# A graph layer's gathers and single rows: 128 rows in every second gather, and single rows loaded in three parts instead of two

## The chip, the cores and the metric

One core of a Trainium2 chip runs the program. The metric is the device time of one execution in microseconds. Four executions of the kernel before took 15,992.88 to 15,995.08 us, median 15,993.74 us. A further execution was taken by the profiler; the trace and the page come from it.

## What is computed

A graph of 50,000 nodes with 128 features and 1,650,000 edges, sorted by target node. Each edge carries its source's row, multiplied by one of two weight matrices, to its target; the sums go through relu, the input is added, and each row is normalized.

```python
Xs = X[src]
m_data = Xs @ W_data.T + b_data
m_ctrl = Xs @ W_control.T + b_control
msg = jnp.where((edge_types == 0)[:, None], m_data, m_ctrl)
agg = jax.ops.segment_sum(msg, dst, num_segments=X.shape[0])
out = jax.nn.relu(agg + (X @ W_self.T + b_self))
x = _layernorm(x + out, axis=-1)
```

Every node also has one edge to itself (a self-loop) among the 1,650,000.

## The kernel before, in words

The kernel sums source rows first and multiplies by the weights afterwards. The edges are cut into blocks of 3234 in their sorted order, so 511 blocks (`NBLK`): 510 full ones and a rest of 7 gathers. A block is two steps (`Q`) of 1617 edges, and a step's edges come to the core in three ways:

- **Gathers.** Twelve (`R`) indirect DMAs on GpSimd's queue (`gathers`, L467, issued at L473) fetch 126 rows each (`SIZES`, L45) into a tile `y`. Six gathers share one slot of ten (`SLOTS`) and form a pass (`PASS`); four passes make a block. TensorE multiplies each gathered set with a one-hot matrix of targets and types (`products`, L484, matmul L492) into `acc`.
- **Fillers.** A self-loop needs no gather, since the node's own row is in the core anyhow. So its place in the gather lists is given to another edge's source: `fill` (L306) puts `F` = 41 edges per step in the places of 41 self-loops among the gathered ones. VectorE does it five blocks ahead (`RAHEAD`), in operations over 26 × 41 = 1066 elements (L316 to L335). Fewer self-loops than F in any step would send the program through a second, general path as well (L568, L936).
- **Single rows.** `S` = 64 edges per step come as 64 ordinary DMAs of 512 bytes. SP's queue issues the first 32 of a step and ScalarE's the other 32 (`TURN`, L423), two blocks ahead (`AHEAD`). `single_rows` (L435) loads 32 row offsets from the SBUF tile `at_x` into registers in one instruction (L442, `TENSOR_LOAD`), then issues 32 DMAs from these registers (L447: a `MOVE` and the DMA for each). VectorE writes the offsets, in bytes, in `offsets` (L433), at the end of the block before. Before the step's last matmul TensorE waits for all of the block's rows (`rows_fetched`, L452) and adds them with one matmul (L498).

`manual_schedule` means that every engine runs its instructions in the order in which the program writes them. The loop at L607 writes, for block b: on SP the load of a later block's own rows (`window`, L403); then, spread over the four passes q = 0 to 3, at q = 0 the weights of block b − 1 (`layer`, TensorE), its mean and variance (`moments`, VectorE), the one-hot matrix of block b + 2 (L409) and single rows of block b + 2, step 0; at q = 1 the square root of block b − 1 on ScalarE (`root`, L547) and the counts (L417); at q = 2 `store` of block b − 1 (VectorE's reciprocal L553 and normalization L555, which need the square root, then the store by SP, L556), the fillers of block b + 5, and single rows of block b + 2, step 1; at q = 3 the offsets of block b + 3. So ScalarE's queue holds, block after block: load, 32 rows, square root, load, 32 rows. SP's holds: own rows, load, 32 rows, store, load, 32 rows.

One more place loads several values into registers: `window` (L397) loads the first nodes of five blocks into SP's registers, in every fifth block; the last time one value is left.

```python
_, regs = nc.values_load_multi_w_load_instructions(
    base_i[0:1, b:b + n], engines=[SP], min_val=0, max_val=N - B,
```

Of the kernel before, what the change touches and what calls it, by code (L numbers as in the profile page):

```python
# [2 lines left out]

# [10 lines left out]
U8 = mybir.dt.uint8  # L14
# [10 lines left out]
ROW = 4 * D  # L25
E = 1650000
P = 128
# [6 lines left out]
R = 12  # L34
W = 60
Q = 2
PASS = 6
B = 112
C = R * Q
F = 41  # L40
S = 64
X = Q * S
R1 = R + 1
C1 = Q * R1
SIZES = [126] * R  # L45
SIZE = sum(SIZES)
CE = Q * SIZE
BE = CE + Q * F + X
NBLK = 2 + (E - CE) // BE
REST = E - CE - (NBLK - 2) * BE  # L50
REST_ROWS = [min(n, max(0, REST - q * SIZE - sum(SIZES[:r]))) for q in range(Q) for r, n in enumerate(SIZES)]
RCH = sum(n > 0 for n in REST_ROWS)
assert len(SIZES) == R and sum(REST_ROWS) == REST
GB = 10
GROUPS = -(-NBLK // GB)
GC = GB * C1
AHEAD = 2
# [17 lines left out]
TBL = GROUPS * GB  # L75
# [3 lines left out]
def plain(b):  # L79

    return b == 0 or b >= NBLK - 1
# [6 lines left out]
def straight(ctx, tc, c, x, x_t, src_t, dst_t, etype_t, src_f, dst_f, etype_f, src_x, dst_first, first_p, out):  # L88
# [13 lines left out]
    nc = tc.nc  # L102
# [21 lines left out]
                   allow_small_or_imprecise_dtypes=True)  # L124
    FILL = Q * F + C1
    small = keep_ps.tile([P, 2 * W + F + 2 * FILL + 2], F32, name="small")
    num_ps, rank_no_ps = small[:, :2 * W], small[:, 2 * W:2 * W + F]
    lists = [small[:, 2 * W + F + i * FILL:][:, :FILL] for i in range(2)]
    sums_at = [small[:Q * F, 2 * W + F + 2 * FILL + i:][:, :1] for i in range(2)]

# [80 lines left out]
    def clear_sums():  # L211
        for t in sums:
            nc.vector.memset(t, 0.0)
            nc.vector.memset(t[0:3, 2, :], 1.0)
            nc.vector.memset(t[0:2, 2, :], 0.0)
# [80 lines left out]
    def spread_out(g):  # L296
        vd_g[g] = dram.tile([GS * F], F32, name="vd")
        nc.sync.dma_start(vd_g[g].rearrange("(s f) -> s f", f=F), vp_g.pop(g))
# [39 lines left out]
    def left_out_columns(b):  # L338

        if not plain(b):  # L340
            pc = sums_at[b % 2]
            nc.tensor.matmul(pc, bys.pop(b).rearrange("p q f -> p (q f)"), ones_b[:, 0:1], start=True, stop=True)  # L342
            pcs[b] = pc

    def left_out_matrix(b):
        if not plain(b):
            z = fil.tile([Q * F, 2, P], BF16, name="z", bufs=RAHEAD + 1)
            at = fil.tile([Q * F, 1], F32, name="at")
            nc.vector.tensor_copy(at, pcs.pop(b))
            nc.vector.tensor_scalar(z.rearrange("p t n -> p (t n)"), node_no, at, None, op0=ALU.is_equal)  # L350
            zs[b] = z
# [22 lines left out]
    def column(k):  # L374
        return k // R * R1 + k % R

    def steps_of(b):
        return [q for q in range(Q) if len(chunks_of(b, q))]
# [8 lines left out]

    idxs = {0: idx0}
    bys, pcs, zs, pls, bases, ats, ys = {}, {}, {}, {}, {}, {}, {}
    ohs, cnts, accs, xTs, pos, hs, mvs, sds = {}, {}, {}, {}, {}, {}, {}, {}  # L390

    BASES = 5

# [12 lines left out]
    def onehot(b):  # L406
        g, i = divmod(b, GB)
        oh = ohp.tile([P, C1, 2 * W], F32, name="oh")
        nc.vector.tensor_tensor(oh, col_g[g][:, i, :, None].to_broadcast([P, C1, 2 * W]),  # L409
                                num_ps[:, None, :].to_broadcast([P, C1, 2 * W]), op=ALU.is_equal)  # L410
        ohs[b] = oh

    def counts(b):

        cnt = ohp.tile([P, Q, 2 * W], BF16, name="cnt")
        with nc.allow_low_precision(reason="whole numbers up to R1"):
            nc.vector.tensor_reduce(cnt, ohs[b].rearrange("p (q r) w -> p q w r", r=R1), AX.X, ALU.add)  # L417
        cnts[b] = cnt
# [1 line left out]


    ROW_SLOTS = AHEAD + 2
    TURN = S // 2  # L423
    RANGE = dict(min_val=0, max_val=(N - 1) * ROW, skip_runtime_bounds_check_because="where a node's row is")
    x_bytes = x.rearrange("n d -> (n d)").bitcast(U8)[None, :]
    fetched = [[tc.alloc_semaphore(f"fetched{j}_{i}") for i in range(ROW_SLOTS)] for j in range(2)]
# [5 lines left out]
            ats[b] = stp.tile([1, X], I32, name="at_x", bufs=AHEAD + 2)  # L432
            nc.vector.tensor_scalar(ats[b], one_g[g][:, i * X:(i + 1) * X], float(ROW), None, op0=ALU.mult)  # L433

    def single_rows(b, q):  # L435

        if q == 0:
            ys[b] = stp.tile([S, Q, D], F32, name="yx", bufs=ROW_SLOTS)
        both = []
        for j, (eng, dma) in enumerate(((SP, nc.sync), (ACT, nc.scalar))):  # L440
            at = j * TURN
            _, rows = nc.values_load_multi_w_load_instructions(  # L442
                ats[b][0:1, q * S + at:q * S + at + TURN], engines=[eng], **RANGE)
            both.append([(dma, fetched[j][b % ROW_SLOTS], at + k, row) for k, row in enumerate(rows)])
        for pair in zip(*both):
            for dma, sem, k, row in pair:
                copy = dma.dma_start(ys[b][k:k + 1, q, :].bitcast(U8), x_bytes[:, bass.ds(row, ROW)])  # L447
                copy.then_inc(sem, 16)
                tc.no_tile_sem_insts.add(copy.ins.name)
                tc.add_to_no_dep_group(f"single{b}", copy.ins)  # L450

    def rows_fetched(b):  # L452

        times = len(range(b % ROW_SLOTS or ROW_SLOTS, b + 1, ROW_SLOTS))
        for j in range(2):
            wait = nc.tensor.wait_ge(fetched[j][b % ROW_SLOTS], 16 * Q * TURN * times)
        tc.declare_fence(wait.ins, group=f"single{b}")


# [7 lines left out]
    def gathers(b, ks):  # L467
# [3 lines left out]
        for k in ks:  # L471
            r = REST_ROWS[k] if b == NBLK - 1 else SIZES[k % R]
            copy = nc.gpsimd.indirect_dma_start(  # L473
# [10 lines left out]
    def products(b, q, ks):  # L484
# [5 lines left out]
        for k in ks:  # L490
            r = REST_ROWS[k] if b == NBLK - 1 else SIZES[k % R]
            nc.tensor.matmul(acc[:, :2, :].rearrange("p t w -> p (t w)"), y[:r, k % PASS, :], ohs[b][:r, column(k), :],  # L492
                             start=k == of_step[0], stop=plain(b) and k == of_step[-1])
        if ks[-1] == of_step[-1]:
            if not plain(b):
                if q == 0:
                    rows_fetched(b)
                nc.tensor.matmul(acc[:, :2, :].rearrange("p t w -> p (t w)"), ys[b][:, q, :],  # L498
                                 ohs[b][:S, q * R1 + R, :], start=False, stop=True)
            for t in range(2):  # L500
# [49 lines left out]
    def store(b):  # L550
        mv = mvs.pop(b)
        rstd = stp.tile([B, 1], F32, name="rstd")
        nc.vector.reciprocal(rstd, sds.pop(b))  # L553
        o = stp.tile([B, D], F32, name="o")
        nc.vector.tensor_scalar(o, hs.pop(b), mv[:, 0:1], rstd, op0=ALU.subtract, op1=ALU.mult)  # L555
        nc.sync.dma_start(out[bass.ds(bases.pop(b), B), :], o)  # L556

    def find_bad():

# [36 lines left out]
    for b in range(1, RAHEAD):  # L596
        fill(b)
        left_out_columns(b)
        left_out_matrix(b)
        if b < AHEAD:  # L600
            onehot(b)
            counts(b)
            for q in range(Q):
                single_rows(b, q)
        if b == 1:
            clear_sums()
    for b in range(NBLK + 1):  # L607
        if b == NBLK - 1:
            find_bad()
        if b + 3 < NBLK:  # L610
            window(b + 3)
        g, i = divmod(b, GB)
        if i == 0 and g + 1 < GROUPS:
            load_edges(g + 1)
        if i == 3 and g + 1 < GROUPS:
            spread_out(g + 1)
        if i == 4 and g + 1 < GROUPS:
            spread_in(g + 1)
        if b > 0:
            add(b - 1, steps_of(b - 1)[-1])  # L620
        if b < NBLK:
            begin_sums(b)
        last = steps_of(b)[-1:]
        for q, (step, ks) in enumerate(passes_of(b)):
            if ks:
                products(b, step, ks)
            if q == 0 and b > 0:
                layer(b - 1)
            if q == 1:
                left_out_numbers(b + 1)  # L630
            if q == 3:
                left_out_columns(b + RAHEAD)
            if ks and step not in last and ks[-1] == chunks_of(b, step)[-1]:
                add(b, step)
            if q == 0 and b > 0:
                moments(b - 1)
            if q == 0 and b + AHEAD < NBLK:
                onehot(b + AHEAD)
            if q == 1 and b > 0:
                root(b - 1)  # L640
            if q == 2 and b > 0:
                store(b - 1)
            if q == 1 and b + AHEAD < NBLK:
                counts(b + AHEAD)
            if q == 2 and i == 2 and g + 1 < GROUPS:
                columns(g + 1)
            if q == 2:
                left_out_rows(b + 1)
                if b + RAHEAD < NBLK:
                    fill(b + RAHEAD)  # L650
            if q == 3:
                left_out_matrix(b + RAHEAD)
                offsets(b + AHEAD + 1)
            if q % 2 == 0 and not plain(b + AHEAD):
                single_rows(b + AHEAD, q // 2)


def general(ctx, tc, c, x, src, dst, etype, out):
# [331 lines left out]
```

## Time and profile before

| | |
|---|---|
| median of four runs | 15,993.74 us |
| the profiled execution | 15,992.88 us |
| its span, first to last instruction | 15,990.9 us |
| blocks, and time from one to the next in mid-run | 511, 31.28 us |
| busy: GpSimd, VectorE, TensorE, ScalarE | 76%, 68%, 52%, 1% |
| single rows issued by SP and by ScalarE | 32,576 each |
| wait of VectorE's reciprocal (L553) for ScalarE's square root | 5.8 us in all |

In the profile an engine's busy time counts its own work. Loads into registers, moves, waits on semaphores and the issue of DMAs run on an engine's queue (written with a q: ACTq is ScalarE's, SPq is SP's) and are not counted as busy, although the engine's next instruction stands behind them. A gather on GpSimd is counted, as DMA_INDIRECT. A group's line gives: code line, engine, operation, out<-in, count, then busy time in us and mean ns of one, then the engine's idle time just before and what ended it ("issue" is time in which the engine waited for nothing that the profile shows). A timeline's line gives start and duration in us.

### The profile page before, as it was taken

The page shows a single profiled execution, that of the slowest core. Times are in us where ns is not written, and L with a number is a line of the kernel's source. Part 1 is how long each engine was busy: PE and PEld are TensorE (multiplying, and loading weights), DVE is VectorE, ACT ScalarE, POOL GpSimd, SP SyncE. Part 2 cuts the span into 40 slices and gives each one's busy share as a digit, 9 for nine tenths or more (in the row PEclk, how much of TensorE's full clock was granted, in tenths as well). Part 3 has the DMA queues.
Part 4 walks back from the last instruction along what each step waited for, and adds up shares of the span by engine and source line. Part 5 has one row for each costly group of instructions (what it writes and reads, how often), then busy time and mean ns, then how long its engine had stood idle before and what let it go on. Part 6 is the DMA issues. An engine that isn't in the chain of part 4 may idle for free.

```text
span 15990.9 us, 246443 instructions
## 1 busy us (share of the span) xinstructions
PE 8293.8 (52%) x35890; PEld 7106.7 (44%) x35891; DVE 10890.9 (68%) x14042; ACT 153.8 (1%) x517; POOL 12232.0 (76%) x12257
## 2 busy tenths in 40 slices
PE   4555555555555555555555555555555555555555
PEld 3444444444444444444444444444444444444444
DVE  8766666666666667666666666666666667666665
ACT  0000000000000000000000000000000000000000
POOL 7777777777777777777777777777777777777777
PEclk6555555555555555555555555555555555555555
DMA  2222222222222222222222222222222222222222
GB/s 62 60 59 59 58 60 58 60 59 58 58 60 59 58 60 58 60 58 60 59 59 59 58 60 58 60 60 59 58 60 59 59 60 58 59 58 59 59 59 56
DMA packets 895864, 944.21 MB, mean 59 GB/s; under 512 B 401739, under 2 KB 715928, under 8 KB 894220
## 3 DMA queue, kind: packets, MB, share of 16 engines
q0 software_dynamic: 587872, 791.74, 20.3%
q1 hardware_dynamic: 240758, 119.60, 3.0%
q10 hardware_dynamic: 65590, 17.01, 0.5%
q14 instruction: 1352, 11.08, 0.2%
q8 instruction: 292, 4.78, 0.1%
HBM read 896.86 MB, written 29.47 MB: 58 GB/s over the span
## 4 chain that ended last, share of the span: by engine, by line
POOL 58%; issue 19%; PE 11%; DMA 6%; DVE 6%; ACTq 0%; POOLq 0%; PEldq 0%; ACT 0%; SPq 0%; DVEq 0%
POOL y L473 58%; PE acc L492 6%; DMA y<-in_x,idx 6%; PE po L531 2%; DVE cnt L417 1%; PE po L529 1%; PE po L528 1%; DVE by L335 1%; DVE h L537 0%; DVE h L538 0%; PE po L527 0%; ACTq L447 0%; DVE new L319 0%; DVE m L316 0%; DVE v_new L323 0%
## 5 line engine op out<-in xcount | busy, mean ns | idle before, releaser
L473 POOL DMA_INDIRECT y<-in_x,idx x12240 | 12223.4, 999 | 3737.3 <-issue 3617.7
L492 PE MATMUL acc<-oh,y 126*128 126x120 f32 x24494 | 5880.4, 429 | 7070.0 <-PEq L480 7035.9
L492 PEld LDWEIGHTS acc<-oh,y 126*128 126x128 f32 x24494 | 5315.6, 326 | 7505.7 <-PEq L480 7460.1
L417 DVE TENSOR_REDUCE cnt<-oh 128x240 bf16<-128x3120 f32 x511 | 2958.1, 5789 | 0.1
L537 DVE COPY h<-po 112x128 f32<-112x128 f32 x511 | 149.1, 292 | 3360.0 <-PE po L531 3352.9
L409 DVE TENSOR_TENSOR oh<-col,small 128x3120 f32<-128x3120 f32 x511 | 1723.1, 3372 | 0.0
L508 DVE TENSOR_TENSOR sums<-acc,sums 128x180 f32 x1021 | 352.6, 345 | 1140.5 <-PE acc L501 1092.3
L335 DVE TENSOR_REDUCE by<-old 128x82 bf16<-128x1066 f32 x509 | 1073.4, 2109 | 17.7
L498 PE MATMUL acc<-oh,yx 64*128 64x120 f32 x2036 | 784.1, 487 | 0.0
L316 DVE TENSOR_TENSOR m<-rk,small 128x1066 f32<-128x1066 f32 x509 | 644.3, 1266 | 17.3
L319 DVE TENSOR_TENSOR new<-m,small 128x1066 f32<-128x1066 f32 x509 | 644.2, 1266 | 17.3
L323 DVE TENSOR_REDUCE v_new<-new 128x26 f32<-128x1066 f32 x509 | 642.9, 1263 | 17.3
L332 DVE TENSOR_TENSOR old<-m,small 128x1066 f32<-128x1066 f32 x509 | 640.1, 1257 | 0.0
L498 PEld LDWEIGHTS acc<-oh,yx 64*128 64x128 f32 x2036 | 501.7, 304 | 212.2 <-issue 208.9
L531 PE MATMUL po<-wmsgT,sums 128*112 128x128 f32 x2044 | 526.3, 402 | 0.0
L531 PEld LDWEIGHTS po<-wmsgT,sums 128*112 128x112 f32 x2044 | 382.4, 257 | 111.4 <-issue 95.0
L342 PE MATMUL small<-ones_b,by 128*82 128x1 bf16 x509 | 112.7, 222 | 591.3 <-DVE by L335 585.1
L342 PEld LDWEIGHTS <-by 128*82 128x82 bf16 x509 | 75.8, 149 | 639.6 <-DVE by L335 635.8
L529 PE MATMUL po<-bias,sums 3*112 3x128 f32 x1022 | 356.9, 446 | 1.1 <-DVE sums L508 1.1
L528 PE MATMUL po<-wselfT,xT 128*112 128x128 f32 x1022 | 318.0, 414 | 0.0
L521 DVE TENSOR_TENSOR sums<-pl,sums 128x336 f32<-128x336 f32 x509 | 258.3, 507 | 85.6 <-DVE sums L508 85.0
L547 ACT ACTIVATE sd<-mv,eps 112x1 f32<-112x1 f32 x511 | 150.6, 295 | 15717.4 <-DVE oh L409 7769.5
(119 smaller groups left out, 4203.5 us busy)
## 6 DMA issues: line engine op xcount, KB each, us to landing
yx<-in_x ACTq DMA_DIRECT2D x32576, 0.5 KB
yx<-in_x SPq DMA_DIRECT2D x32576, 0.5 KB
y<-in_x,idx POOLq DMA_INDIRECT x12240
xT<-in_x_t SPq DMA_DIRECT2D x511, 56.0 KB
out<-o SPq DMA_DIRECT2D x511, 56.0 KB
vf_all<-vd SPq DMA_DIRECT2D x52, 410.0 KB
s<-in_src_t SPq DMA_DIRECT2D x52, 130.0 KB
d<-in_dst_t SPq DMA_DIRECT2D x52, 130.0 KB
```

Of the source, the lines that this page charges most:

```text
L316: nc.vector.tensor_tensor(m, rk_g[g][:, i, :, None].to_broadcast([P, C1, F]), rank_no_ps[:, None, :].to_broadcast([P, C1, F]), op=ALU.is_e ...
L319: nc.vector.tensor_tensor(new.rearrange("p (q r) f -> p q r f", r=R1), m.rearrange("p (q r) f -> p q r f", r=R1), vf.rearrange("p (q f) -> ...
L323: nc.vector.tensor_reduce(v, new, AX.X, ALU.add)
L332: nc.vector.tensor_tensor(old, m, cb[:, :, None].to_broadcast([P, C1, F]), op=ALU.mult)
L335: nc.vector.tensor_reduce(by, old.rearrange("p (q r) f -> p q f r", r=R1), AX.X, ALU.add)
L409: nc.vector.tensor_tensor(oh, col_g[g][:, i, :, None].to_broadcast([P, C1, 2 * W]), num_ps[:, None, :].to_broadcast([P, C1, 2 * W]), op=AL ...
L417: nc.vector.tensor_reduce(cnt, ohs[b].rearrange("p (q r) w -> p q w r", r=R1), AX.X, ALU.add)
L473: copy = nc.gpsimd.indirect_dma_start(out=y[:r, k % PASS, :].bitcast(U8), out_offset=None, in_=x_rows, in_offset=bass.IndirectOffsetOnAxis ...
L492: nc.tensor.matmul(acc[:, :2, :].rearrange("p t w -> p (t w)"), y[:r, k % PASS, :], ohs[b][:r, column(k), :], start=k == of_step[0], stop= ...
L498: nc.tensor.matmul(acc[:, :2, :].rearrange("p t w -> p (t w)"), ys[b][:, q, :], ohs[b][:S, q * R1 + R, :], start=False, stop=True)
L529: nc.tensor.matmul(po, a[0:3, 2, :B], bias, start=False, stop=False)
L531: nc.tensor.matmul(po, a[:, t, :B], c["wmsgT"][:, t * D:(t + 1) * D], start=False, stop=t == 1)
```

## The change

Six gathers of a step keep 126 rows and six, every second one, take 128: `SIZES` sums to 1524 instead of 1512. `F` is 42 instead of 41. Single rows are 74 a step instead of 64: SP issues 36 of them and ScalarE 38. The offsets of a block now lie by engine: both steps' 72 for SP first, then both steps' 76 for ScalarE. Each engine's list is cut into three parts (`LOADS`), of 24 on SP and of 25, 25 and 26 on ScalarE; each part is one load into registers and its DMAs, written at q = 0, 1 and 2. The square root of the block before stands between ScalarE's first and second part. The store of block b − 1 is written at q = 3 instead of q = 2, so behind SP's third part. The block has 3280 edges, and there are 504 blocks, the last with 4 gathers.

```diff
-F = 41
-S = 64
+F = 42
+TURNS = (36, 38)
+S = sum(TURNS)
+LOADS = 3
...
-SIZES = [126] * R
+SIZES = [126, P] * (R // 2)
...
-    def single_rows(b, q):
-
-        if q == 0:
+    def single_rows(b, part):
+
+        if part == 0:
             ys[b] = stp.tile([S, Q, D], F32, name="yx", bufs=ROW_SLOTS)
         both = []
         for j, (eng, dma) in enumerate(((SP, nc.sync), (ACT, nc.scalar))):
-            at = j * TURN
-            _, rows = nc.values_load_multi_w_load_instructions(
-                ats[b][0:1, q * S + at:q * S + at + TURN], engines=[eng], **RANGE)
-            both.append([(dma, fetched[j][b % ROW_SLOTS], at + k, row) for k, row in enumerate(rows)])
-        for pair in zip(*both):
-            for dma, sem, k, row in pair:
-                copy = dma.dma_start(ys[b][k:k + 1, q, :].bitcast(U8), x_bytes[:, bass.ds(row, ROW)])
+            n = Q * TURNS[j]
+            k0, k1 = part * n // LOADS, (part + 1) * n // LOADS
+            at = Q * sum(TURNS[:j])
+            _, rows = nc.values_load_multi_w_load_instructions(ats[b][0:1, at + k0:at + k1], engines=[eng], **RANGE)
+            both.append([(dma, fetched[j][b % ROW_SLOTS], *divmod(k0 + k, TURNS[j]), sum(TURNS[:j]), row)
+                         for k, row in enumerate(rows)])
+        for pair in zip_longest(*both):
+            for dma, sem, q, k, at, row in filter(None, pair):
+                copy = dma.dma_start(ys[b][at + k:at + k + 1, q, :].bitcast(U8), x_bytes[:, bass.ds(row, ROW)])
...
-        nc.sync.dma_start(out[bass.ds(bases.pop(b), B), :], o)
+        os_[b] = o
+
+    def store_rows(b):
+        nc.sync.dma_start(out[bass.ds(bases.pop(b), B), :], os_.pop(b))
...
-            if q % 2 == 0 and not plain(b + AHEAD):
-                single_rows(b + AHEAD, q // 2)
+            if q < LOADS and not plain(b + AHEAD):
+                single_rows(b + AHEAD, q)
+            if q == LOADS and b > 0:
+                store_rows(b - 1)
...
-        ones[1:] = steps[:, :, SIZE + F:].reshape(TBL - 1, X)
+        single = steps[:, :, SIZE + F:]
+        ones[1:] = np.concatenate([single[:, :, sum(TURNS[:j]):][:, :, :n].reshape(TBL - 1, Q * n)
+                                   for j, n in enumerate(TURNS)], axis=1)
```

## The prediction, made before the changed kernel was run

> **What bounds the kernel now.** I read the page's group list first. GpSimd issues one gather per 126 rows:
>
> ```profile
> L473 POOL DMA_INDIRECT y<-in_x,idx x12240 | 12223.4, 999 | 3737.3 <-issue 3617.7
> ```
>
> One gather is 0.999 us busy and 3737.3 / 12240 = 0.305 us idle that nothing but its own issue ends, so 1.304 us each; 24 to a block make 31.29 us, and 511 blocks (the last with 7 gathers) make 12,247 × 1.304 = 15,970 of the 15,990.9 us span. GpSimd's queue is the bound, with about 21 us around it. VectorE is busy 68%, TensorE 52%.
>
> Next I asked what is nearly as full. The busy shares leave out queue work, and the single rows are queue work, so I read ScalarE's timeline over one block, from one square root (L547) to the next:
>
> ```profile
> 8035.66 0.29 ACT L547 ACTIVATE sd<-mv,eps 112x1 f32<-112x1 f32 x1 [30.37 <-DVE oh L409]
> 8037.96 10.35 ACTq L447 DMA_DIRECT2D yx<-in_x  x32
> ...
> 8056.53 10.64 ACTq L447 DMA_DIRECT2D yx<-in_x  x32
> 8067.27 0.30 ACT L547 ACTIVATE sd<-mv,eps 112x1 f32<-112x1 f32 x1 [31.31 <-DVE oh L409]
> ```
>
> Of the 31.61 us, 21.0 go to issuing 64 rows. Ahead of each 32 rows stands one load of 32 offsets into registers. Line 442 by engine (duration min/median/max in ns):
>
> ```profile
> L442 ACTq TENSOR_LOAD <-at_x x1018: 2111/2145/2405, 16.5 to 15887.2; - x170
> L442 SPq TENSOR_LOAD <-at_x x1018: 1864/2066/2309, 26.8 to 15897.4; - x170
> ...
> L433 DVE TENSOR_SCALAR at_x<-one_g x1: 206/206/206, 8054.0 to 8054.0; 1x128 int32<-1x128 int32 x1
> ```
>
> The two loads of this block took 2.16 and 2.13 us. ScalarE stood still from 8048.31, its row 32, to 8054.21, when VectorE's offsets for the next block (L433) were there: 5.90 us. Its work is 25.7 us a block, and 5.6 us (18%) is all the room it has.
>
> **The loads, which decide.** Three parts instead of two need loads that begin at other values. One other load of several values stands in the trace: line 397 loads five block starts on SP every fifth block, and the last time one (number 510). At 156.4 us apart, counting back from the last, these begin at values 260, 265, 270, 275, 280 and 510:
>
> ```profile
> L397 SPq TENSOR_LOAD <-base_i x1: 834/834/834, 8057.4 to 8057.4; - x1
> L397 SPq TENSOR_LOAD <-base_i x1: 1335/1335/1335, 8214.1 to 8214.1; - x1
> L397 SPq TENSOR_LOAD <-base_i x1: 1334/1334/1334, 8369.9 to 8369.9; - x1
> L397 SPq TENSOR_LOAD <-base_i x1: 1332/1332/1332, 8527.0 to 8527.0; - x1
> L397 SPq TENSOR_LOAD <-base_i x1: 799/799/799, 8682.9 to 8682.9; - x1
> L397 SPq TENSOR_LOAD <-base_i x1: 532/532/532, 15879.7 to 15879.7; - x1
> ```
>
> Five values that begin at a multiple of four take 0.8 us, five that begin elsewhere 1.33. All 103 divide so: 26 take 754 to 949 ns, 76 take 1322 to 1464. One value takes 532 (472 at line 934 on SP, 463 on ScalarE). I read it thus: from a multiple of four, four values come in one step; from any other start each value is a step of its own. Five single steps: 532 + 4 × 200 = 1332. An aligned 32 is eight steps: on SP (2066 − 472) / 7 = 228 ns a step, on ScalarE (2145 − 463) / 7 = 240. The present loads begin at 0, 32, 64 and 96.
>
> The changed loads: SP takes 24 values from 0, 24 and 48, all multiples of four. ScalarE's part of the list begins at 2 × 36 = 72, and its 76 are cut at 25 and 50: 25 values from 72, **25 from 97, 26 from 122**. The last two begin off a multiple of four.
>
> **The sum for ScalarE, per block.** A single step on ScalarE isn't in the trace. SP's single step is 200 (from 532) or 216 (from 472 up to the median 1336) against its 228 for a group: 0.88 to 0.95. I take 0.92 × 240 = 220 ns; bounds 200 (SP's row) and 240 (ScalarE's group). From 72: six fours and one, 0.463 + 6 × 0.240 = 1.90 us. From 97: 0.463 + 24 × 0.220 = 5.74. From 122: 0.463 + 25 × 0.220 = 5.96. Loads 13.6 us, where two took 4.3. Rows: 32 took 10.50 on average, a further one 0.3235 ((10.35 − 0.47) / 31 and (10.64 − 0.47) / 31, the first being 0.47 long), so 25 take 8.24 and 26 take 8.56: 25.04. The rest of the block above (31.61 less rows, loads and wait) is 0.43; with a third part 0.6. **Together 39.2 us** against GpSimd's 31.29, so ScalarE's queue becomes the bound. Nothing covers it: behind the late square root wait VectorE's reciprocal (L553) and, in order, all of VectorE's fills and indices.
>
> **The whole run.** Block size goes from 3234 to 2 × (1524 + 42 + 74) = 3280 edges, so NBLK from 511 to 504, of which 502 have single rows: 502 × 39.24 = 19,698 us. ScalarE begins at 16.5; rows of two and a third blocks (89 us) are done before the first square root, which stands at 116 for VectorE's start-up and stays there: 19,698 − 89 + 116 = 19,725. After its last row the span ran 91 us on; with gathers far ahead I take 50 (30 to 91). That is a span of 19,775. The profiled execution took 15,992.9, 2.0 beyond its span and 0.9 below the median of 15,993.7: 19,780.
>
> **The other edits cost nothing beneath that.** Gathers: 503 × 24 + 4 = 12,076, 171 fewer, worth 223 us if GpSimd were still the bound. A 128-row gather isn't in the trace. The nearest are 126 rows (997 ns median) and the last, 114 rows (1132): by rows 126 to 128 adds 16, by the 1132 it could be 135 more, by rows per engine (9 to 8) 111 less. I take +16; at +135 a block's gathers make 31.29 + 12 × 0.135 = 32.9, hidden by 39.2. SP: three loads of 24 (six steps, 0.472 + 5 × 0.228 = 1.61), 72 rows at 0.3235 with 0.05 for each first, one store, one xT: near 30 us, hidden also. Its store (a 0.34 us issue) moves behind the third part and no longer waits for o; it stays ahead of the next block's xT, which has five buffers, and holds o, one of three buffers, some 20 us longer. VectorE: the four 1066-element operations and L335 grow by 1/41, 0.17 us of 21. TensorE: 74 rows for 64 under one unchanged matmul form.
>
> [...]
>
> **Rivals.** (a) *The start doesn't matter in long loads*: line 397 has only five values. Then 25, 25 and 26 take 1.90, 1.90 and 2.14; ScalarE needs 25.04 + 5.94 + 0.6 = 31.58, level with GpSimd's 31.29. By ScalarE 15,853 − 74 + 116 + 52 = 15,947; by GpSimd 15,994 − 223 = 15,771, with +16 ns on 6,038 gathers 15,868. I put it at **15,860**, faster. It decides wherever ScalarE's block stays under 15,994 / 504 = 31.7 us. (b) *A wrong start costs a fixed 0.54 us* (1335 − 799): loads 1.90 + 2.44 + 2.68, block 32.66, run 16,395 − 76 + 168 = **16,490**. Against both: the 200-ns fit from one to five values and to 32. (c) *The longer list itself stands off a multiple of four in memory*, so that the load from 72 is slow as well: 43.1 a block, **21,700**. Against: 148 values are 37 fours, so slots keep their places. (d) *The change doesn't run its own path*: fewer than 42 self-loops among a step's gathered edges would start the general path as well. I counted them in the inputs: at least 42 in each of the 1,004 steps, mean 46.2. No chance given.
>
> **Chances.** Forecast 0.85, (a) 0.07, (b) 0.06, (c) 0.02. The forecast's ends: steps of 200, rows from the 10.35 part (24.7), rest 0.5, tail 30: block 37.8, 19,040 us; steps of 240, rows from the 10.64 part (25.35): 40.5, tail 91: 20,470. I give 0.95 that these hold if the mechanism is right, so 0.81 of all. Measurement tells 0.2% (32 us) from no change: faster 0.06, same 0.01, slower 0.93, from (a) and the rest.
>
> **What would show it.** Line 442 on ScalarE in two heights, a third of them near 1.9 us and two thirds at 5.3 to 6.7, SP's all below 2.1; square roots 39 us apart; no wait of ScalarE for L433; reciprocal L553 waiting for L547 thousands of us in all (5.8 now); GpSimd busy about 60%, held by slots. Wrong if all of line 442 stays near 2 us, or if square roots stand 31 us apart.

## The result and the profile after

The changed kernel takes 19,740.9 us (median of 8 runs) against 15,994.2 us for the kernel before: a ratio of 1.2346, 95% interval 1.2334 to 1.2359. The profiled execution took 19,740.0 us with a span of 19,738.3 us. The forecast was 19,780.

On the page of the changed kernel I read the chain that ended last and two groups: gathers and the reciprocal that needs ScalarE's square root.

```profile
ACTq 85%; issue 13%; ACT 1%; DVE 1%; PE 0%; DMA 0%; SPq 0%; DVEq 0%
ACTq L451 52%; ACTq L446 33%; ACT sd L551 1%; DVE cnt L420 0%; PE acc L496 0%; DVE by L338 0%; ACTq L551 0%; DVE new L322 0%; DVE m L319 0%; DVE v_new L326 0%; DVE old L335 0%; DVE oh L412 0%; PE po L535 0%; DMA first_i<-in_dst_first 0%; PE po L533 0%
...
L477 POOL DMA_INDIRECT y<-in_x,idx x12072 | 11795.8, 977 | 7861.2 <-PE acc L496 4141.7
...
L557 DVE RECIPROCAL rstd<-sd 112x1 f32<-112x1 f32 x504 | 82.6, 164 | 6821.3 <-ACT sd L551 6821.3
```

The chain is ScalarE's queue, 85% of it: 52% its rows (L451), 33% its loads (L446). GpSimd now waits 4142 us for slots that TensorE hasn't freed, and VectorE waits 6821 us in all for the square root, 13.6 us a block, where it waited 5.8 us in the whole run before. ScalarE's timeline from one square root to the next:

```profile
7996.84 0.29 ACT L551 ACTIVATE sd<-mv,eps 112x1 f32<-112x1 f32 x1 [39.13 <-issue]
8002.55 33.49 ACTq L451 DMA_DIRECT2D yx<-in_x  x76
8036.15 0.29 ACT L551 ACTIVATE sd<-mv,eps 112x1 f32<-112x1 f32 x1 [39.01 <-issue]
```

39.3 us lie between the two, with no wait for VectorE's offsets. The first row comes 5.7 us after the square root because a load stands there. All loads of single rows' offsets, min/median/max in ns:

```profile
L446 ACTq TENSOR_LOAD <-at_x x1506: 1893/5602/6067, 17.0 to 19698.3; - x189
L446 SPq TENSOR_LOAD <-at_x x1506: 1420/1677/1900, 27.3 to 19666.7; - x189
```

SP's loads all stay below 2 us. ScalarE's fall into three heights by their place in the block: from value 72 a median of 2.00 us, from 97 5.60 (never below 5.48), from 122 5.85.

### The profile page after: what moved, and what is told of

The parts are those of the page before. It is cut to its first block, busy times and chain, and to the rows that moved or that the text cites. A ratio compares the mean times of both kernels' runs of the same rounds, so it can differ in the third digit from the quotient of the medians.

```text
span 19738.3 us, 264109 instructions
## 1 busy us (share of the span) xinstructions
PE 5765.4 (29%) x35388; PEld 5416.9 (27%) x35389; DVE 10761.7 (55%) x13843; ACT 151.6 (1%) x510; POOL 11801.1 (60%) x12086
## 4 chain that ended last, share of the span: by engine, by line
ACTq 85%; issue 13%; ACT 1%; DVE 1%; PE 0%; DMA 0%; SPq 0%; DVEq 0%
ACTq L451 52%; ACTq L446 33%; ACT sd L551 1%; DVE cnt L420 0%; PE acc L496 0%; DVE by L338 0%; ACTq L551 0%; DVE new L322 0%; DVE m L319 0%; DVE v_new L326 0%; DVE old L335 0%; DVE oh L412 0%; PE po L535 0%; DMA first_i<-in_dst_first 0%; PE po L533 0%
## 5 line engine op out<-in xcount | busy, mean ns | idle before, releaser
L477 POOL DMA_INDIRECT y<-in_x,idx x12072 | 11795.8, 977 | 7861.2 <-PE acc L496 4141.7
L496 PE MATMUL acc<-oh,y 126*128 126x120 f32 (+1 forms) x24152 | 4194.7, 345 | 0.1
L496 PEld LDWEIGHTS acc<-oh,y 126*128 126x128 f32 (+1 forms) x24152 | 3952.4, 255 | 0.3 <-PE po L588 0.2
L338 DVE TENSOR_REDUCE by<-old 128x84 bf16<-128x1092 f32 x502 | 1065.0, 2122 | 17.4
L319 DVE TENSOR_TENSOR m<-rk,small 128x1092 f32<-128x1092 f32 x502 | 648.5, 1292 | 17.1
L322 DVE TENSOR_TENSOR new<-m,small 128x1092 f32<-128x1092 f32 x502 | 648.3, 1291 | 17.1
L326 DVE TENSOR_REDUCE v_new<-new 128x26 f32<-128x1092 f32 x502 | 648.0, 1291 | 17.1
L335 DVE TENSOR_TENSOR old<-m,small 128x1092 f32<-128x1092 f32 x502 | 644.4, 1284 | 0.0
L502 PE MATMUL acc<-oh,yx 74*128 74x120 f32 x2008 | 461.3, 318 | 0.0
L502 PEld LDWEIGHTS acc<-oh,yx 74*128 74x128 f32 x2008 | 382.9, 237 | 0.0
```

The costliest lines, as they stand in the source:

```text
L319: nc.vector.tensor_tensor(m, rk_g[g][:, i, :, None].to_broadcast([P, C1, F]), rank_no_ps[:, None, :].to_broadcast([P, C1, F]), op=ALU.is_e ...
L322: nc.vector.tensor_tensor(new.rearrange("p (q r) f -> p q r f", r=R1), m.rearrange("p (q r) f -> p q r f", r=R1), vf.rearrange("p (q f) -> ...
L326: nc.vector.tensor_reduce(v, new, AX.X, ALU.add)
L338: nc.vector.tensor_reduce(by, old.rearrange("p (q r) f -> p q f r", r=R1), AX.X, ALU.add)
L477: copy = nc.gpsimd.indirect_dma_start(out=y[:r, k % PASS, :].bitcast(U8), out_offset=None, in_=x_rows, in_offset=bass.IndirectOffsetOnAxis ...
```

## The experiments

**Theory** (my reading of these durations): a load into registers that begins at a multiple of four takes four values a step; 32 took 2.15 us in the kernel before. One that begins elsewhere takes one value a step, about 0.21 us each, (5.602 − 0.463) / 24. This puts ScalarE's queue above GpSimd's. **Rivals:** the third part or an odd count makes loads slow; a wrong start costs a fixed sum; it isn't the loads but the rows. In the traces of the first four runs (e1 to e4), SP's and ScalarE's queues stood still for some 0.7 us between instructions, thousands of times each, and the kernel before took 22,914 us beside them. Why is open. So of these four only the durations of loads and gathers are used, and the kernels were run again on a later occasion. The kernel before took 15,970 to 16,002 us beside these later runs, and each ratio is to the one beside it.

### The start alone, in the kernel before

```diff
+            off[b] = stp.tile([1, X + 4], I32, name="at_off", bufs=AHEAD + 2)
+            nc.vector.tensor_scalar(off[b][:, 1:1 + X], one_g[g][:, i * X:(i + 1) * X], float(ROW), None, op0=ALU.mult)
...
-                ats[b][0:1, q * S + at:q * S + at + TURN], engines=[eng], **RANGE)
+                (off[b][0:1, 1:] if j else ats[b])[0:1, q * S + at:q * S + at + TURN], engines=[eng], **RANGE)
```

The first time:

> The kernel before, with a second copy of the offsets written one place later for ScalarE (one more VectorE operation of about 0.2 us a block), so that ScalarE's two loads of 32 begin at 33 and 97 of a tile instead of 32 and 96; SP's loads, counts, rows and gathers stay. Theory (from a start off a multiple of four each value is a step): 32 values take 0.463 + 31 x 0.214 = 7.1 us instead of 2.15, ScalarE's block is 25.85 + 2 x 4.95 = 35.75 us, and the run is ScalarE's at 509 x 35.75 + 80 = 18,280 us. Rival (a wrong start costs a fixed 3.6 us, the difference of 5.60 and 2.00): 33.05 us a block, 16,900 us. Rival (the count or the third part decided): 15,994 us, loads at 2.15.

22,509 us against 22,914 (0.982, 0.980 to 0.984), with pauses in its queues; but ScalarE's loads had a median of 7.0 us. Once more:

> The kernel before, with ScalarE's two loads of 32 offsets beginning one place later (33 and 97 of a tile that VectorE writes beside the other, 0.2 us a block); SP's loads, counts, rows and gathers stay. Theory (from a start off a multiple of four each value is a step of about 0.21 us): loads 7.1 us instead of 2.15, ScalarE's block 25.85 + 2 x 4.95 = 35.75 us, run 509 x 35.75 + 80 = 18,280 us. Rival (a wrong start costs a fixed 3.6 us, 5.60 less 2.00): 33.05 a block, 16,900 us. Rival (a third part or a count that isn't a multiple of four made the changed kernel's loads slow): 15,980 us. Where the queues pause as in the first four runs, only the loads tell.

18,259 us in the profiled run, 18,357 the median of two; ratio 1.147 (1.140 to 1.154). Its loads:

```profile
L445 ACTq TENSOR_LOAD <-at_off x1018: 6997/7088/7302, 17.1 to 18212.8; - x170
L445 SPq TENSOR_LOAD <-at_x x1018: 1864/2080/2259, 27.4 to 18214.1; - x170
```

And its waits, with total us, times and longest:

```profile
DVE rstd L556 <- ACT sd L550: 5209.5, 510, 21.8
```

Beside one more VectorE operation of 0.2 us a block, which writes the second tile, nothing but the place of the first value differs from the kernel before. The count is still 32 and there are two parts, and the load takes 7.09 us instead of 2.15. (7.088 − 0.463) / 31 = 0.214 us a value, the same as (5.602 − 0.463) / 24 in the changed kernel. A square root came every 35.76 us, where the sum had given 35.75. This shows the start as the cause, a price of 0.214 us for each value, and the step from the loads through ScalarE's queue to the time. That each value is a step of its own is a reading of this price. The fixed price, the third part and the odd count fall as causes.

### The changed kernel with its cuts at multiples of four

```diff
-            k0, k1 = part * n // LOADS, (part + 1) * n // LOADS
+            k0, k1 = (n if p == LOADS else p * n // LOADS // 4 * 4 for p in (part, part + 1))
```

> The changed kernel with ScalarE's 76 offsets cut at 24 and 48 instead of 25 and 50, so that its three loads begin at 72, 96 and 120, all multiples of four; nothing else differs. Theory (the start decides): ScalarE's loads of 24, 24 and 28 take 6, 6 and 7 steps, about 1.75, 1.75 and 2.0 us instead of 2.00, 5.60 and 5.85, so its block falls from 39.22 to 31.3 us; GpSimd's, with 997 and 957 ns gathers in turn as the changed kernel's trace shows them, is 24 x 1.283 = 30.8; the run is ScalarE's, 502 x 31.3 less 73 for the rows issued before the first square root, plus 116 and about 60, near 15,800 us. Rival (the third part, or the longer list, makes loads slow whatever their start): 19,740 us as in the changed kernel. Rival (the count decides, 24 being a multiple of four and 25 not): the same fall as the theory, which the run with a moved start tells apart.

24,809 us against 22,914 (1.083, 1.081 to 1.085), again with pauses; loads at 1.7, 1.7 and 2.0 us. Then:

> The changed kernel with ScalarE's offsets cut at 24 and 48 once more, since in the first runs of it, and in the kernel before beside them (22,914 us), SP's and ScalarE's queues stood still for some 0.7 us between rows, thousands of times, and bounded every kernel. Where those pauses are missing (kernel before near 15,994 us): theory (the start decides) 15,800 us, ScalarE's block 31.3 us, loads near 1.7, 1.7 and 2.0 us; rival (a third part or a longer list is slow whatever its start) 19,740 us. Where they are there again, the loads alone tell: 1.7 to 2.0 us by the theory, 5.6 and 5.9 by the rival.

16,513.8 us against 15,971.5 (1.034, 1.032 to 1.036). Its loads:

```profile
L446 ACTq TENSOR_LOAD <-at_x x1506: 1662/1766/2238, 17.2 to 16456.6; - x189
L446 SPq TENSOR_LOAD <-at_x x1506: 1418/1678/1907, 27.6 to 16476.5; - x189
```

The loads fall as the theory said, and with them 3,227 us, 86% of the loss. But 15,800 was expected, and the kernel is still slower than before. The chain of this run names other holders:

```profile
SPq 32%; DVE 20%; DMA 17%; issue 13%; ACTq 12%; PE 5%; PEld 0%; ACT 0%; DVEq 0%; PEldq 0%
```

### What is left: the place of the store

SP's timeline in this run showed a stop in every tenth block:

```profile
8263.89 0.34 SPq L563 DMA_DIRECT2D out<-o  x1
8264.47 0.36 SPq L406 DMA_DIRECT2D xT<-in_x_t  x1
...
8267.16 0.38 SPq L174 DMA_DIRECT2D df<-in_dst_f  x1
8279.46 0.28 SPq L174 DMA_DIRECT2D tf<-in_edge_type_f  x1
```

The store, moved to the end of the block, is followed at once by the loads of the next ten blocks' edges. SP's DMAs that aren't single rows take turns on eight semaphores (118 and 120 to 126 in the traces of the kernel before and of the changed one), so the last of these, the ninth from the store, waits until the store has landed: 12 us. In all:

```profile
SPq L174 <- DMA out<-o: 608.3, 49, 14.1
```

The next kernel writes the store ahead of the third part, as before the change.

```diff
                 store(b - 1)
+                store_rows(b - 1)
...
-            if q == LOADS and b > 0:
-                store_rows(b - 1)
```

> The changed kernel with ScalarE's cuts at 24 and 48 and the store of the block before written ahead of the third part again (q = 2). In the run with the cuts alone (16,514 us) SP stood 12 us in every tenth block at L174, since the ninth DMA from the store reuses the store's semaphore and waits for its landing. Theory (this stop sets part of the time, as SP has no slack): the stop goes, 51 x 12.3 = 630 us at the most, so 15,890 to 16,200 us. Rival (ScalarE's 32.2 us a block bind anyhow): 16,400 to 16,514 us.

16,515.7 us against 16,002.1 (1.032, 1.030 to 1.034), the same as without it. The wait of L174 went down to 36 us in all, and the time didn't move: the rival held.

```profile
SPq L174 <- DMA out<-o: 36.4, 46, 2.5
```

The chain is now ScalarE's:

```profile
ACTq 64%; issue 15%; DVE 15%; PE 5%; ACT 1%; DMA 0%; DVEq 0%; SPq 0%; PEldq 0%
ACTq L451 53%; ACTq L446 12%; DVE cnt L420 3%; PE acc L496 3%; DVE by L338 2%; DVE m L319 1%; DVE new L322 1%; DVE v_new L326 1%; DVE old L335 1%; ACT sd L551 1%; PE po L535 1%; PE po L533 1%; PE po L532 0%; DVE pl L370 0%; DVE st L544 0%
```

In mid-run ScalarE never waits here, and a block takes it 32.8 us where I had summed 31.3. Its loads are as expected; its rows aren't. From one row's issue to the next the mean is 354 ns, in the kernel before 333, in the changed kernel 335. The usual distance is the same (a median of 318 ns), but 27% of the rows come later than 345 ns, against 8 to 9% in those two. SP's rows went the same way, 349 for 330 ns. It happened in the three kernels in which both queues issued nearly all the time (348 ns in the run before this one, 354 here, 351 in the last kernel below). That a row of the one queue waits for a row of the other isn't shown, and the traces speak against it: in this run ScalarE's rows with no row of SP's issued in the 345 ns before them come later still (367 ns on average, the others 349), and in h2_rows64 below, where 90% of ScalarE's rows have one of SP's so near, the mean is 338. What does go with it is a longer transfer. The queue of ScalarE's rows, first in the changed kernel, then here (packets, MB, the time that they took as a share of 16 engines' span):

```profile
q10 hardware_dynamic: 76742, 19.88, 0.5%
...
q10 hardware_dynamic: 76742, 19.88, 1.4%
```

A 512-byte packet of this queue takes 31 ns on average in the kernel before, 30 in the changed kernel and 74 here. What makes it longer is open.

### What is left: the number of rows

```diff
-TURNS = (36, 38)
+TURNS = (32, 32)
```

> The changed kernel with ScalarE's and SP's parts cut at multiples of four and 64 single rows a step again, 32 for each queue, still in three loads (20, 20 and 24), with 42 fillers and the store behind the third part: 507 blocks, 12,150 gathers of 126 and 128 rows in turn. Theory (with the starts mended, what is left of the loss, 16,514 us, is the 76 rows of ScalarE's queue, 32.2 us a block and more): ScalarE needs 25.9 + 0.7 = 26.6 us and SP 28, GpSimd's 30.8 bind, 12,150 x 1.282 + 24 = 15,600 to 15,660 us. Rival (the third load, the longer list or the place of the store costs on its own): 16,000 us and more.

15,624.7 us against 15,969.8 (0.978, 0.977 to 0.980). With 64 rows, aligned starts and everything else of the change in place, GpSimd is the bound again:

```profile
POOL 55%; issue 18%; PE 11%; DMA 8%; DVE 7%; ACTq 0%; POOLq 0%; PEldq 0%; DVEq 0%; ACT 0%; SPq 0%
```

Its loads begin at 0, 20 and 40 on SP and at 64, 84 and 104 on ScalarE, of which 20 and 84 are multiples of four and not of eight. ScalarE's 20 values take 1.43 us (median) from 64 and 1.45 from 84:

```profile
L446 ACTq TENSOR_LOAD <-at_x x1515: 1418/1451/1990, 16.9 to 15527.1; - x190
L446 SPq TENSOR_LOAD <-at_x x1515: 1197/1459/1896, 27.2 to 15519.7; - x190
```

So the ten added rows a step cost 16,514 − 15,625 = 889 us, although they save three blocks of 507. Third load, moved store and 42 fillers cost nothing here: the kernel of the next section does without them and takes 0.979 of the time before, this one 0.978.

### The gathers alone

```diff
-SIZES = [126] * R
+SIZES = [126, P] * (R // 2)
```

> The kernel before with the gathers' sizes alone changed: 126 and 128 rows in turn, 41 fillers, 64 single rows in two loads as before; 507 blocks, 12,158 gathers. The changed kernel's trace shows 957 ns for the 128-row gather and 997 for the 126-row one, but GpSimd was not its bound. Theory (the shorter time is the 128-row gather's own and holds when GpSimd is the bound): 12,158 x (0.977 + 0.305) + 24 = 15,610 us, 2.4% less than before. Rival (it is short only because GpSimd's queue has pauses): 997 ns for both, 12,158 x 1.304 + 24 = 15,878. Rival (prediction's middle, 16 ns more per 128-row gather): 15,975.

23,108 us against 22,914 (1.009, 1.007 to 1.010), with pauses; the gathers took 1,001 and 959 ns in turn. Then:

> The kernel before with the gathers' sizes alone changed, 126 and 128 rows in turn: 507 blocks, 12,158 gathers, 41 fillers, 64 single rows in two loads. Theory (the 128-row gather's 957 ns are its own and gain time where GpSimd is the bound): 12,158 x (0.977 + 0.305) + 24 = 15,610 us. Rival (the shorter gather is given back in waits for rows or slots): 15,878 us, 12,158 x 1.304 + 24.

15,660.2 us against 16,002.1 (0.979, 0.977 to 0.980), the profiled run 15,629.7; the rival's 15,878 falls. The gathers of the kernel before (min/median/max in ns), then those of this one in turn, of 126 and 128 rows:

```profile
L473 POOL DMA_INDIRECT y<-in_x,idx x12240: 992/997/1860, 3.2 to 15961.8; - x198
...
7999.86 1.00 POOL L473 DMA_INDIRECT y<-in_x,idx  x1 [0.30 <-issue]
8001.17 0.96 POOL L473 DMA_INDIRECT y<-in_x,idx  x1 [0.31 <-issue]
```

And with 128 rows everywhere (`SIZES = [P] * R`):

> The kernel before with 128 rows in every gather, 41 fillers and 64 single rows in two loads as before; 503 blocks, 12,069 gathers. Theory (a 128-row gather takes 957 ns whatever stands before it): 12,069 x (0.957 + 0.305) + 24 = 15,255 us, 4.6% less than before; ScalarE's 25.85 and SP's 27.2 us a block stay below GpSimd's 30.3. Rival (it needs the 126-row gather between, so that one behind another over the same 16 engines waits): 128-row gathers above 1.0 us, the run at 15,600 to 15,800 us or more.

23,538 against 22,914 (1.027, 1.025 to 1.029), with pauses; gathers of 944 ns. Then:

> The kernel before with 128 rows in every gather: 503 blocks, 12,069 gathers, 41 fillers, 64 single rows in two loads. Theory (944 ns behind one another, as the first run of it showed beside a paused queue): 12,069 x (0.944 + 0.305) + 24 = 15,100 us, 5.5% below before; SP's block, 27.2 us, is below GpSimd's 29.98. Rival (SP's and ScalarE's rows become dearer as the gathers come denser, and bind): 15,300 us and more, with GpSimd waiting for TensorE.

15,147.7 us against 16,002.1 (0.947, 0.945 to 0.948), the fastest kernel of the study. Its gathers, all of 128 rows in the first line, in the second the last block's, which end with one of 86:

```profile
L473 POOL DMA_INDIRECT y<-in_x,idx x12048: 941/947/1647, 3.2 to 15103.0; - x198
...
L473 POOL DMA_INDIRECT y<-in_x,s x21: 943/947/1438, 15104.2 to 15129.2; - x21
```

A 128-row gather is 40 ns shorter than one of 126 when the two take turns (957 against 997 in the changed kernel), and 50 ns when all have 128 (947). That gain is there in the changed kernel too, and idle there. Of g3's 854 us, 178 gathers fewer than 12,247 give 232, and 50 ns on 12,069 about 600.

### A version with all of it

128 rows in every gather, `TURNS = (34, 36)`, cuts at multiples of four, 42 fillers:

> 128 rows in every gather (940 to 944 ns in the first run of such a kernel), 42 fillers, 70 single rows a step (34 on SP, 36 on ScalarE) in three parts that all begin at multiples of four; 501 blocks, 12,018 gathers. Theory: GpSimd is the bound at 24 x (0.944 + 0.305) = 30.0 us a block, since SP's 68 rows need about 29.4 and ScalarE's 72 about 29.8: 12,018 x 1.249 + 24 = 15,035 us, 6% below the kernel before. Rival (the queues of SP and ScalarE, at 98% and 99%, bind before GpSimd does): 15,200 to 15,400 us, with GpSimd's idle time waiting for TensorE.

15,702.6 us against 15,971.5 (0.983, 0.982 to 0.985): 1.7% faster than the kernel before, slower than g3 with its 64 rows.

```profile
SPq 27%; ACTq 20%; DVE 18%; DMA 16%; issue 14%; PE 5%; ACT 0%; PEld 0%; DVEq 0%; PEldq 0%
```

GpSimd could have done with 30.0 us a block; a block took 31.3, with SP and ScalarE at 27% and 20% of the chain. So the rival's mechanism fits, but the time lies above its range of 15,200 to 15,400 as well: rows came late again, 351 ns apart on ScalarE and 342 on SP, which neither sum had in it.

## Why the prediction was right, step by step

- **The bound moves to ScalarE's queue through two loads off a multiple of four.** Shown, by the three heights and by g1. I had 1.90, 5.74 and 5.96 us, measured were 2.00, 5.60 and 5.85; a step was 214 ns for my 220. The choice between SP's 200 and ScalarE's 240 by SP's ratio came out nearly right.
- **39.24 us a block.** Measured 39.22 in mid-run: loads 13.46 for 13.60, all else 25.76 for 25.64. The two errors have opposite signs, so that the sum is right to 0.02 us is in part luck; each alone is 1% or less.
- **The ends.** The first square root stood at 116.0 as said. The tail was too long: the last row was issued at 19,713.0, 25 us before the end, where I took 50 within 30 to 91: outside that range. That is most of the 40 us between forecast and result.
- **The 128-row gather.** I took 16 ns more, within 111 less and 135 more; it is 40 less, 957 against 997. The 111 is 997 / 9, the price of one row of 9. The packets show shares of 9 rows and of 8 (last section); that a share is one engine's isn't shown, and 40 isn't that price. It was hidden here either way, as said, but in rival (a) the sign mattered.
- **Rival (a), that the start doesn't matter,** fell with g1. Its price was wrong as well: mended starts give 16,514 us, not 15,860, since its rows, priced at 0.3235 us from one to the next, came 0.348 us apart there and 0.354 in g4. So the change was slower for two reasons, and the forecast named only the larger. It had the smaller in sight as "31.58, level with GpSimd's 31.29", and priced rows from a kernel in which ScalarE rested 5.6 us a block.
- **Rival (b), a fixed price,** fell: 32 values cost 4.94 us more, not 3.6 or 0.54. **(c)** fell: the load from 72 stayed at 2.00.
- **The price of a value.** On ScalarE a value off a multiple of four took 214 ns, and one of the 32 aligned ones 54, (2.145 − 0.463) / 31.
- **The rest:** SP's queue, summed to near 30 us, needed 30.8 and was hidden; GpSimd was busy 60%, held by slots.

## What to carry to other kernels

A queue that shows 1% busy can be the bound, as ScalarE's was here with 85% of the chain: sum its register loads, moves and DMA issues per block, and ask how much rest it has before giving it more. Cut lists for register loads at multiples of four values; the two wrong starts cost 3,227 us, the ten added rows 889. When a change has several parts, time each alone: here the one that gained, the gathers, was idle behind the one that lost.

## What the runs showed of the hardware that was not expected

- Durations of gathers: 12 rows 892 ns (the last of the changed kernel), 48 rows 887 (the last of f2), 126 rows 997, 114 rows 1132 (the last of the kernel before), 86 rows 1438 (the last of g3), 128 rows 944 to 957. Fewer rows took longer here: 114 of them 135 ns more than 126 in the same kernel. The packets of the traces show how a gather is divided, a row being 512 bytes: 12 packets of 512 bytes for 12 rows, 14 of 4,096 and 14 of 512 for each gather of 126 (in the kernel before 171,444 of 512 for 12,246 gathers), 16 of 4,096 for 128 rows, 16 of 1,536 for 48, and 6 and 2 of 1,536 beside those of 4,096 for the ends of 114 and 86. I read them as 12, 14, 16, 16, 6 and 2 equal shares, of 1, 9, 8, 3, 19 and 43 rows, cut into packets of at most 8 rows. An estimate from these durations and shares: those with fewer than 16 shares lie on 879 + 13.1 ns per row of a share (892, 997, 1128, 1442), and those of 16 shares 25 to 40 ns under it. Which engines took the packets isn't shown, nor why a row of a share should cost 13 ns.
- In the changed kernel TensorE is busy 29% instead of 52%; its granted clock was 0.605 of full speed instead of 0.536, and its matmul of a gather (L496, before L492) took 345 ns instead of 429.
